# The end of a two-stage transformer kernel, ordered by hand: a change to the last two of 96 units

## The chip, the cores and the metric

One core of one Trainium2 chip. The metric is the device time of one execution in microseconds (us). The engines are TensorE (PE), VectorE (DVE), ScalarE (ACT), GpSimd (POOL) and SyncE (SP, which here issues DMAs only).

## The reference, cut to what matters

```python
def reference(...):          # x is (4, 512, 128) float32
    x = x + attention(layernorm(x), Wq, Wk, Wv, Wr)     # 16 heads of 64, penalty -50 above the diagonal
    x = x + layers(layernorm(x), ...)                   # six layers, as follows
    return x

for i in range(6):
    x = attn_layer(shift_tokens(x), Wqkv[i], q_scale[i], k_scale[i], Wo[i]) + x
    x = ffn_layer(shift_tokens(x), ln_g[i], ln_b[i], W1[i], b1[i], W2[i], b2[i]) + x

def attn_layer(...):         # q and k: norm per head, scale, rotary; windows of 32 queries
    ...                      # see their own and the previous 32 keys; softmax; product with V; Wo

def ffn_layer(x, ...):
    xn = (x - mu) / sqrt(var + 1e-05) * g + bln
    a, gate = split(xn @ W1 + b1)                       # 341 and 341 columns
    return a * gelu(gate) @ W2 + b2
```

`shift_tokens` takes the upper 64 of the 128 features from the token before. A batch is 512 tokens, that is 4 tiles of 128.

## The kernel before, in words

The order of instructions is the order in which the Python code issues them: the body runs under `tc.manual_schedule()`, each engine works off its own queue in that order, and semaphores, placed by the framework, hold an instruction until its data are there and its buffer is free.

The first stage (global attention) runs until about 560 us (its last transposes of probabilities, L315, start at 557 us). The second stage is cut into 96 units: 6 layers x 4 batches x 4 tiles of 128 tokens. `slot(n, ...)` issues one step of a software pipeline: for unit n the scores, exponents, their transposes, the product with V (`times_v`, in two halves) and the transposes of its result (`transpose_o`); for unit n-1 the product with Wo (`project_out_2`) and the residual; for unit n+1 the transposes of q and k; for unit n+2 the projections and norms. The feed-forward part of a batch (`Ffn`) is spread over seven slots behind the batch's last residual: `shift`, `mean`, `var`, `scale` (the layer norm), three GEGLU chunks of 128, 128 and 85 of the 341 columns, and `out` (the product with W2 and the residual). In the last layer `out` ends with `finish`: the sum with the first stage's output (`x1T`), four transposes, a copy and the output DMA. The loop runs on to slot 102, so the last slots hold ever less work: slot 94 and 95 belong to the last two units, 96 to 102 to the last batch's feed-forward alone.

Lines of before that are spoken of below: L80 to L86, the reciprocal square root by three Newton steps (4 instructions each, `rsqrt`), on VectorE for the feed-forward norms; L94 to L98 mean, subtraction and square; L103 the variance (products with one column); L111 the broadcast of the inverse root by transposes; L115, L117 the scaled result hT; L147 to L149 the shift by one token on GpSimd; L513 and L521 GpSimd's rotary sum and scaling; L585, L588 transposes and their copies by ScalarE; L604 the carry of 32 keys on GpSimd; L612, L623 scores (mask, then products); L633, L635 maximum and subtraction; L641 exponents; L655 the product with V; L664, L665 its division; L680, L688 product with Wo and residual; L713, L714 the two products of a GEGLU chunk (gate, value); L716 Gelu; L718 the gate's multiplication; L727 and L729 product with W2 and residual; L738, L741, L743, L744 the sum, transposes, copy and DMA of `finish`. ScalarE loads a function table (ACT_TABLE_LOAD) when it goes from exponents to Gelu or back.

PSUM: `one_t` hands out two banks in turn (transposes, means, variances, Wo products); `two_t(k)` hands out three pairs of banks, counted from `part[0]`. A taker waits until the former content of its bank has been read.

Of the kernel before, what the change touches and what calls it, by code (L numbers as in the profile page):

```python
# [15 lines left out]
P = 128  # L16
# [16 lines left out]
def body(ctx: ExitStack, tc: tile.TileContext, a, out: bass.AP):  # L33
# [41 lines left out]
    def rsqrt(v, n, eng):  # L75

        y = small.tile([P, n], F32, tag=f"y{n}", name="y")
        t = small.tile([P, n], F32, tag=f"yt{n}", name="yt")
        ti = t.bitcast(I32)
        nc.vector.tensor_scalar(ti, v.bitcast(I32), 1, None, ALU.logical_shift_right)  # L80
        nc.vector.tensor_scalar(y.bitcast(I32), ti, -1.0, 1597463007.0, ALU.mult, ALU.add)  # L81
        for k in range(3):
            eng.tensor_tensor(t, y, y, ALU.mult)  # L83
            eng.tensor_tensor(t, t, v, ALU.mult)
            eng.tensor_scalar(t, t, -0.5, 1.5, ALU.mult, ALU.add)
            eng.tensor_tensor(y if k < 2 else v, y, t, ALU.mult)  # L86

    def layernorm_steps(state, bank, inT, outT, g=None, b=None, eng=nc.vector):

        def mean():
            m = bank()
            mm(m, lhsT=avg, rhs=inT(), start=True, stop=True)  # L94
            xc = state["xc"] = tmpt()
            nc.vector.tensor_tensor(xc, inT(), m, ALU.subtract)
            sq = state["sq"] = tmpt()
            nc.scalar.activation(sq, xc, AF.Square)  # L98

        def var():  # L100
            v = bank()
            for t in range(NT):
                mm(v[:, t : t + 1], lhsT=state["sq"][:, t * P : (t + 1) * P], rhs=avg[:, 0:1], start=True, stop=True)  # L103
            rs = state["rs"] = small.tile([P, NT], F32, tag="rs", name="rs")
            nc.vector.tensor_scalar(rs, v[:, 0:NT], EPS, None, ALU.add)
            rsqrt(rs, NT, eng)

        def scale():
            bc = bank()
            for t in range(NT):  # L110
                nc.tensor.transpose(  # L111
                    bc[:, t * P : (t + 1) * P], state["rs"][:, t : t + 1].to_broadcast([P, P]), ident
                )
# [31 lines left out]
    def shift_into(dst, src):  # L145
# [3 lines left out]
        nc.gpsimd.tensor_copy(dst[HD:P, 1:S], src[HD:P, 0 : S - 1])  # L149
# [543 lines left out]
    class Ffn:  # L693
        def __init__(self, i, b):
            self.i, self.b, self.us, self.st = i, b, [], {}
# [4 lines left out]
                lambda: s2.tile([P, S], F32, tag="hT", name="hT", bufs=2),  # L700
                vecs[:, i, 0:1],
                vecs[:, i, 1:2],
            )

        def shift(self):
            self.xs = tmpt()
            shift_into(self.xs, xT[self.b])

        def chunk(self, f):
            i, (f0, fn), h = self.i, FCH[f], self.st["h"]  # L710
            w1 = ffn_w[0][0]
            gp = two_t(0, "ps_proj")
            mm(gp[0:fn, 0, :], lhsT=w1[:, DH + f0 : DH + f0 + fn], rhs=h, start=True, stop=True)  # L713
            mm(gp[0:fn, 1, :], lhsT=w1[:, f0 : f0 + fn], rhs=h, start=True, stop=True)  # L714
            g = tmpt()
            nc.scalar.activation(g[0:fn, :], gp[0:fn, 0, :], AF.Gelu, bias=vecs[0:fn, i, 6 + f : 7 + f])  # L716
            u = tmpt()
            nc.vector.scalar_tensor_tensor(  # L718
                u[0:fn, :], gp[0:fn, 1, :], vecs[0:fn, i, 3 + f : 4 + f], g[0:fn, :], ALU.add, ALU.mult
            )  # L720
            self.us.append(u)

        def out(self):
            w2 = ffn_w[0][1]
            y = two_t(0, "ps_proj")[:, 0, :]
            for f, (f0, fn) in enumerate(FCH):
                mm(y, lhsT=w2[0:fn, f, :], rhs=self.us[f][0:fn, :], start=(f == 0), stop=(f == len(FCH) - 1))  # L727
            xn = new_xT()
            nc.vector.scalar_tensor_tensor(xn, y, vecs[:, self.i, 2:3], xT[self.b], ALU.add, ALU.add)  # L729
            xT[self.b] = xn  # L730
            if self.i + 1 == L:
                self.finish(xn)
            elif self.b + 1 == B:
                ffn_w[0] = load_ffn(self.i + 1)

        def finish(self, xn):
            fin = tmpt()
            nc.vector.tensor_tensor(fin, x1T[self.b], xn, ALU.add)  # L738
            op = one_t()
            for t in range(NT):  # L740
                nc.tensor.transpose(op[:, t * P : (t + 1) * P], fin[:, t * P : (t + 1) * P], ident)  # L741
            ot = tmpt()
            nc.scalar.copy(ot, op)  # L743
            nc.sync.dma_start(  # L744
                out=out[self.b].rearrange("(t p) e -> p t e", p=P),
# [57 lines left out]
    def slot(n, now, last):  # L803
# [4 lines left out]
        T = n % NT  # L808
# [20 lines left out]
        if now and T > 0:  # L829
            (now.mean, now.var, now.scale)[T - 1]()  # L830
        if now and T == 0:
            now.shift()
# [34 lines left out]
        if now and T == 3:  # L867
            now.chunk(0)
        if last:
            (lambda: last.chunk(1), lambda: last.chunk(2), last.out)[T]()  # L870
# [3 lines left out]
    with tc.manual_schedule():  # L874
        begin(units[0])
        ffns = {}
        late = norm_x1(one_t, B - 1)
        first_slot()
        for n in range(-1, len(units) + NT + 3):
            if 1 <= n < 4:  # L880
                late[n - 1]()
            q = n // NT - 1
            if n % NT == 0 and 0 <= q < L * B:
                ffns[q] = Ffn(units[n - 1].i, units[n - 1].b)
            slot(n, ffns.get(q), ffns.pop(q - 1, None) if n % NT == 2 else ffns.get(q - 1))
# [93 lines left out]
```

## Time and profile before

| what | value |
|---|---|
| median of 3 runs (lowest, highest) | 2278.62 us (2278.29, 2281.74) |
| profiled execution | 2281.5 us, span of its instructions 2279.7 us |
| mean granted TensorE clock | 0.993 |
| busy PE, PEld, DVE, ACT, POOL | 2178.0, 1435.6, 1729.1, 1347.6, 1451.3 us |
| chain that ended last | PE 63%, DVE 9%, issue 2%, ACT 1% |
| last copy of a result ends | 2276.5 us; its DMA is issued at 2276.5 us |

The page cuts the span into 40 slices of 57 us. PE's digit is 9 in all but the first and the last, where it is 7. A PE that is "busy" all the time isn't at its peak, since matmuls are pipelined; but in the second stage little other than PE's own order ends waits. The span starts with the first instruction; 1.8 us of the execution lie around it.

### The profile page before, as it was taken

Reading aid. Unit: us, or ns where it says so; the run is one execution under the profiler, and the core shown is the slowest. Engines: PE = TensorE matmul, PEld = TensorE weight load, DVE = VectorE, ACT = ScalarE, POOL = GpSimd, SP = SyncE. Lnnn points to the kernel's source line nnn. Section 1 sums busy time; section 2 is a strip of 40 time slices with the busy share of each in tenths; the row PEclk is TensorE's granted clock in tenths of the full one; section 3 lists DMA queues with packets and bytes.
Section 4 is the critical chain, followed back from the end, with each engine's and each line's share of the span. In section 5 each row is a group of like instructions: output and inputs, shape, how many; then the busy total and the mean of one; then the engine's idle time right before and its main releaser. Section 6 shows DMA issues by size and latency. Waiting matters only on the chain.

```text
span 2279.7 us, 82205 instructions
## 1 busy us (share of the span) xinstructions
PE 2178.0 (96%) x35088; PEld 1435.6 (63%) x35088; DVE 1729.1 (76%) x2800; ACT 1347.6 (59%) x2550; POOL 1451.3 (64%) x1981
## 2 busy tenths in 40 slices
PE   6999999999999999999999999999999999999997
PEld 3555555555566666666666666666666666666664
DVE  3776667767778787878887788878888878888774
ACT  3665655655455656666566666666656666666562
POOL 1544545455877677767677777677776667766760
PEclk8999999999999999999999999999999999999998
DMA  3000000000322233232322323222332223222220
GB/s 115 1 1 1 1 1 1 1 1 1 75 70 64 63 88 75 58 75 68 87 67 64 77 70 91 64 62 69 85 85 56 72 63 88 73 67 70 65 56 15
DMA packets 91029, 125.74 MB, mean 55 GB/s; under 512 B 25390, under 2 KB 39468, under 8 KB 90668
## 3 DMA queue, kind: packets, MB, share of 16 engines
q1 hardware_dynamic: 90236, 118.92, 21.1%
q8 instruction: 279, 4.57, 0.9%
q10 hardware_dynamic: 432, 1.57, 0.2%
q14 instruction: 82, 0.67, 0.1%
HBM read 20.31 MB, written 1.05 MB: 9 GB/s over the span
## 4 chain that ended last, share of the span: by engine, by line
PE 63%; DVE 9%; issue 2%; ACT 1%; POOL 0%; POOLq 0%; ACTq 0%
PE ps_proj L477 19%; PE ps_one L585 14%; PE ps_one L680 7%; PE ps_att L655 6%; PE ps_att L623 6%; PE ps_proj L713 3%; PE ps_proj L714 3%; PE ps_proj L727 2%; DVE yt L80 2%; DVE t L502 1%; DVE rot L498 1%; PE ps_att L612 1%; PE ps_one L94 1%; PE ps_one L103 1%; DVE yt L83 1%
## 5 line engine op out<-in xcount | busy, mean ns | idle before, releaser
L513 POOL TENSOR_TENSOR rot<-rot,t 128x1024 f32<-128x1024 f32 x192 | 453.8, 2364 | 197.5 <-DVE t L502 185.9
L477 PE MATMUL ps_proj<-wqkv,xs 128*128 128x512 f32 x1152 | 553.3, 603 | 4.3 <-DVE t L502 2.8
L304 POOL TENSOR_TENSOR pr<-pr,den 128x1024 f32<-128x1024 f32 x128 | 240.9, 1893 | 266.9 <-DVE den L301 258.6
L488 ACT ACTIVATE sq<-ps_proj 128x1024 f32<-128x1024 f32 x192 | 196.8, 1025 | 356.7 <-PE ps_proj L477 324.5
L521 POOL TENSOR_TENSOR rot<-rot,ss 128x1024 f32<-128x1024 f32 x192 | 365.2, 1902 | 14.9
L477 PEld LDWEIGHTS ps_proj<-wqkv,xs 128*128 128x128 f32 x1152 | 198.1, 190 | 166.1 <-issue 146.5
L493 DVE TENSOR_REDUCE ss<-sq 128x16 f32<-128x1024 f32 x192 | 233.1, 1214 | 46.9 <-ACT sq L488 46.3
L498 DVE TENSOR_TENSOR rot<-ps_proj,lt 128x1024 f32<-128x1024 f32 x192 | 233.6, 1217 | 0.0
L502 DVE TENSOR_TENSOR t<-ps_proj,lt 128x1024 f32<-128x1024 f32 x192 | 233.2, 1215 | 0.4 <-POOL rot L513 0.4
L290 ACT ACTIVATE pr<-ps_sc,nm 128x128 f32<-128x128 f32 (+3 forms) x448 | 220.1, 507 | 20.0 <-DVE nm L279 16.7
L279 DVE TENSOR_REDUCE nm<-ps_sc 128x2 f32<-128x1024 f32 x128 | 156.0, 1219 | 91.0 <-PE ps_sc L267 91.0
L585 PE MATMUL ps_one<-ident,rot 128*128 128x128 f32 x1536 | 211.3, 280 | 5.9 <-issue 4.4
L680 PEld LDWEIGHTS ps_one<-aT,wo 128*128 128x128 f32 x1536 | 186.3, 192 | 45.3 <-issue 44.5
L83 POOL TENSOR_TENSOR yt<-y 128x32 f32<-128x32 f32 (+1 forms) x309 | 72.9, 236 | 210.5 <-DVE y L81 194.3
L633 DVE TENSOR_REDUCE mx<-ps_att 128x16 f32<-128x1024 f32 x96 | 117.5, 1224 | 102.3 <-PE ps_att L623 102.2
L680 PE MATMUL ps_one<-aT,wo 128*128 128x128 f32 x1536 | 187.3, 275 | 0.4 <-ACT aT L588 0.4
L585 PEld LDWEIGHTS ps_one<-ident,rot 128*128 128x128 f32 x1536 | 165.3, 141 | 25.3 <-issue 7.1
L319 ACT COPY pT<-ps_pt 128x512 f32<-128x512 f32 x128 | 75.5, 590 | 176.2 <-PE ps_pt L315 176.2
L655 PEld LDWEIGHTS ps_att<-vw,pT 64*32 64x32 f32 x9216 | 103.5, 105 | 93.4 <-ACT pT L588 54.0
L567 ACT COPY vt<-ps_proj 128x512 f32<-128x512 f32 x192 | 103.2, 590 | 93.6 <-PE ps_proj L477 91.6
L315 PEld LDWEIGHTS ps_pt<-ident,pr 128*128 128x128 f32 x1024 | 117.6, 142 | 56.7 <-issue 47.6
L655 PE MATMUL ps_att<-vw,pT 64*32 64x65 f32 x9216 | 129.0, 225 | 24.2 <-DVE t L502 13.4
(134 smaller groups left out, 4062.3 us busy)
## 6 DMA issues: line engine op xcount, KB each, us to landing
vw<-vt SPq DMA_DIRECT2D x1152, 65.0 KB
vw_first<-vt SPq DMA_DIRECT2D x336, 65.0 KB
wqkv<-in_wqkv_dram SPq DMA_DIRECT2D x18, 512.0 KB
wo<-in_wo_dram SPq DMA_DIRECT2D x6, 512.0 KB
w<-in_w_dram SPq DMA_DIRECT2D x6, 341.0 KB
xr<-in_x_dram SPq DMA_DIRECT2D x4, 256.0 KB
out_dram<-tmp_t SPq DMA_DIRECT2D x4, 256.0 KB
w<-in_w_dram SPq DMA_DIRECT2D x12, 64.0 KB
```

The costliest lines, as they stand in the source:

```text
L290: nc.scalar.activation(self.pr[:, h, cols], self.sc[:, h, cols], AF.Exp, bias=self.nm[:, part_, h : h + 1], accum_out=self.den[:, part_, h ...
L304: nc.gpsimd.tensor_tensor(self.pr, self.pr, self.den[:, 0].unsqueeze(2).to_broadcast([P, 2, S]), ALU.mult)
L477: mm(p[:, c, :], lhsT=u.xs[:, u.T * P : (u.T + 1) * P], rhs=wpart[j][:, c * 512 : (c + 1) * 512], start=True, stop=True,)
L488: nc.scalar.activation(u.sq, u.p[j], AF.Square)
L493: nc.vector.tensor_reduce(u.ss[:, j * HEADS : (j + 1) * HEADS], heads(u.sq), AX.X, ALU.add)
L498: nc.vector.tensor_tensor(heads(t0), heads(pf), lt[:, u.T, 2 * j].unsqueeze(1).to_broadcast([P, HEADS, HD]), ALU.mult)
L502: nc.vector.tensor_tensor(t1.rearrange("p (h t d) -> p h t d", t=2, d=half), pf.rearrange("p (h t d) -> p h t d", t=2, d=half)[:, :, ::-1, :],
L513: nc.gpsimd.tensor_tensor(u.r[j], u.r[j], u.t1, ALU.add)
L521: nc.gpsimd.tensor_tensor(heads(u.r[j]), heads(u.r[j]), u.ss[:, j * HEADS : (j + 1) * HEADS].unsqueeze(2).to_broadcast([P, HEADS, HD]), AL ...
L585: nc.tensor.transpose(tp[:, c * P : (c + 1) * P], src[:, (4 * g + c) * P : (4 * g + c + 1) * P], ident)
L655: mm(o[j * W : (j + 1) * W, h, c * (HD + 1) : (c + 1) * (HD + 1)], lhsT=u.pT[h * HD : (h + 1) * HD, 4 * g + c, j * W : (j + 1) * W], rhs=u ...
L680: mm(y[:, 0:P], lhsT=wo_w[0][:, c, :], rhs=u.aT[:, c, :], start=(c == 0), stop=(c == NC - 1))
```

## The change

Slots -1 to 93 issue what they issued before (but for the sum in `out`, which is now written in place). Slot 94 changes, and what follows is written out in `tail()`:

- In slot 94 the `out` of batch index 1 moves from the end of the slot to just behind the variance of batch index 2 (`plan(norm, end - 2, seq.var, ...)`). The scores of unit 95 come at that slot's end (`early_scores`), ahead of the result transposes (`finish`) of batch index 1 and of `transpose_o` of unit 94.
- The inverse root of batch index 2's norm, and those of the last batch, run on GpSimd (two integer instructions of each stay on VectorE).
- Batch index 2 (`seq`): its first GEGLU chunk comes right behind unit 95's product with V, its first gate behind that unit's divisions and result transposes; chunks 1 and 2 come later, `out` and `finish` later still.
- The last batch is cut in two: `most`, its first three tiles (384 columns), normed while unit 95 is at work, and `last`, the fourth tile (128 columns), normed between the chunks. The fourth tile's shift is two copies on ScalarE.
- Output: `finish` is split from `out`; the last three result transposes come last. The last batch's output is two DMAs, of 3 tiles and of 1.

The diff at its core:

```diff
-    def layernorm_steps(state, bank, inT, outT, g=None, b=None, eng=nc.vector):
+    def layernorm_steps(state, bank, inT, outT, g=None, b=None, eng=nc.vector, nt=NT, temp=tmpt):
...
-        def __init__(self, i, b):
+        def __init__(self, u, t0=0, nt=NT, temp=tmpt, pair=None, eng=None):
...
         def shift(self):
-            self.xs = tmpt()
-            shift_into(self.xs, xT[self.b])
+            n, c0 = self.nt * P, self.t0 * P
+            xs, src = self.temp()[:, 0:n], self.u.xn
+            if c0 == 0:
+                shift_into(xs, src[:, 0:n], n)
+            else:
+                nc.scalar.copy(xs[0:HD, :], src[0:HD, c0 : c0 + n])
+                nc.scalar.copy(xs[HD:P, :], src[HD:P, c0 - 1 : c0 + n - 1])
+            self.xs = xs
...
+            def gate():
+                nc.vector.scalar_tensor_tensor(
+                    u[0:fn, :], gp[0:fn, 1, 0:n], vecs[0:fn, i, 3 + f : 4 + f], g[0:fn, :], ALU.add, ALU.mult
+                )
+
+            if apart:
+                return gate
+            gate()
...
-        def finish(self, xn):
-            fin = tmpt()
-            nc.vector.tensor_tensor(fin, x1T[self.b], xn, ALU.add)
-            op = one_t()
+        def finish(self):
+            n, nt, t0, xn = self.nt * P, self.nt, self.t0, self.xn
+            op = one_t()[:, 0:n]
...
+        third, seq = f, Ffn(units[end - NT - 1], eng=nc.gpsimd)
+        plan(norm, end - 4, seq.shift)
+        plan(norm, end - 3, seq.mean)
...
+        most = Ffn(units[end - 2], 0, NT - 1, big, halves, nc.gpsimd)
+        last = Ffn(units[end - 1], NT - 1, 1, big, sixths, nc.gpsimd)
+        u, prev = units[end - 1], units[end - 2]
+
+        def early_scores():
+            part[0] = 0
+            scores(u)
+
+        plan(norm, end - 2, seq.var, *geglu.pop(end - 2))
+        plan(geglu, end - 2, early_scores, third.finish)
+
+        def tail():
+
+            exponents(u)
+            seq.scale()
+            project_out_2(prev)
+            residual(prev)
+            most.shift()
+            transpose_p(u)
+            most.mean()
+            part[0] = 1
+            times_v(u, 0)
+            times_v(u, 1)
+            part[0] = 0
+            gate = seq.chunk(0, 0, True)
+            transpose_o(u)
+            gate()
+            most.var()
+            project_out_2(u)
+            residual(u)
+            last.shift()
+            seq.chunk(1, 1)
+            last.mean()
+            most.scale()
+            last.var()
+            seq.chunk(2, 2)
+            for k in range(2):
+                most.chunk(k, k)
+            last.scale()
+            most.chunk(2, 2)
+            seq.out(0, True)
+            for k in range(3):
+                last.chunk(k, (k + 1) % 3)
+            seq.finish()
+            most.out(1, True)
+            last.out(2, True)
+            most.finish()
+            last.finish()
+
         first_slot()
-        for n in range(-1, len(units) + NT + 3):
+        for n in range(-1, end - 1):
             if 1 <= n < 4:
                 late[n - 1]()
...
+            slot(n, norm.get(n, ()), geglu.get(n, ()))
+        tail()
```

`third` is batch index 1 (its feed-forward is the third from the end), `seq` batch index 2. The chunks' and norms' tiles of the last batch live in buffers of the projections that are idle by then (`big`, `halves`, `sixths`).

## The prediction

> **What bounds the kernel now.** I read the busy shares and slices first, then the built order of both kernels, then stage windows, clock, chain and timeline of the end. Every instruction and wait before TensorE's L103 of the second-to-last unit (it ends at 2219.80 us) is the same in both, but for one addition written in place. So only 2219.80 to 2279.7 can change: the 17.0, 14.2, 25.5 and 3.2 us of these windows (columns after the two times' sum: PE, PEld, DVE, ACT, POOL busy; last but two the granted clock):
>
> ```profile
> 2219.80:2236.80 17.00, 14.04 (x308) 10.38 (x308) 8.59 (x22) 6.02 (x10) 3.93 (x4) 0.80 0.06 17
> 2236.80:2251.00 14.20, 10.71 (x185) 8.59 (x186) 6.34 (x10) 5.06 (x7) 0.00 (x0) 1.00 0.01 2
> 2251.00:2276.50 25.50, 19.72 (x56) 8.41 (x54) 11.03 (x28) 5.22 (x8) 1.21 (x2) 0.93 0.03 10
> 2276.50:2279.70 3.20, 0.00 (x0) 0.00 (x0) 0.00 (x0) 0.00 (x0) 0.00 (x0) 0.60 0.27 82
> ```
>
> PE is busy 44.5 of 59.9 us; elsewhere it is near 99%. The chain shows where it is late (start, length, what):
>
> ```profile
> 2230.45 0.76 DVE xT L729
> 2231.23 0.70 DVE tmp_t L738
> ...
> 2243.89 1.60 issue
> 2245.49 0.45 PE ps_att L655 x25
> ...
> 2264.01 2.08 PE ps_proj L713 x2
> 2266.09 1.33 PE ps_proj L714 x2
> ```
>
> Result transposes stand in PE's queue ahead of the next work and wait for VectorE (1.66 us before 2232.07, 2.13 before 2261.56); the last batch's hT lets PE idle 1.36 us before 2264.01. A second loss is the clock:
>
> ```profile
> 2223.00:2223.50 0.50, 0.50 (x38) 0.50 (x37) 0.47 (x2) 0.00 (x0) 0.50 (x2) 0.50 0.00 0
> 2235.00:2235.50 0.50, 0.50 (x54) 0.50 (x41) 0.00 (x0) 0.16 (x1) 0.00 (x0) 0.50 0.47 142
> 2264.00:2265.00 1.00, 0.99 (x1) 0.50 (x2) 0.00 (x0) 0.00 (x0) 0.00 (x0) 0.50 0.70 222
> ```
>
> It is 0.50 in three spells: 2222.5 to 2225.6, 2232.8 to 2236.3, 2263.5 to 2266.5. So L655 took 1.98 us instead of 0.86, and L713 with L714 3.2 instead of 1.72.
>
> **What the Trainium skill says.** "TensorE: Matmul & The Clock Gate", Part 1: a free-running window of 3413 ns with too little activity is followed by half clock. The trace agrees: the spells' starts are 10.2 and 30.7 us apart, 3.0 and 9.0 such windows, and each follows a stretch with idle time and transposes. "ScalarE: Activation LUTs", What ACT_TABLE_LOAD costs: about 1283 ns; here 1283 (L716, x67), hidden in the end (2242.21, its Gelu at 2247.89). "GPSIMD Engine Reference", Specifications: VectorE instructions with two SBUF inputs contend with GpSimd. Here too:
>
> ```profile
> 2220.05 1.36 DVE L80 TENSOR_SCALAR yt<-rs 128x4 int32<-128x4 int32 x1
> 2221.65 1.74 DVE L83 TENSOR_TENSOR yt<-y 128x4 f32<-128x4 f32 x1
> ```
>
> They last until GpSimd's L513 and L521 end.
>
> **The change, part by part.** Durations: 128x512 product 0.86, so 384 columns 0.65; 128 columns 0.233 (L680: 8 in 1.86); transpose 0.11; N=1 product 0.24; PE's last issue to the reader's start 0.28; VectorE 0.69 (two tensors), 0.75 (gate), 0.55, 384 columns less 0.13; ACT copy 0.59, Gelu 0.69.
>
> *Slot of the second-to-last unit.* L727's product goes behind L103, where PE was idle 0.99 us. From 2219.80: 2.58 (product), 0.44 + 0.28 (first transposes), 0.59 + 0.04 (copy), L655 0.86, q 0.88, L655 0.86, k 0.88: 2227.3. kT's copies add 0.4, the moved-up scores 1.95 (0.34 + 1.61): 2229.6, against 2236.76. The 7.2 us are the late transposes' wait and order (2.2), VectorE's 12-step square root that held L664 to 2225.64, and two cold spells. On GpSimd the 12 steps (200 ns each and 80 gap, 3.3) stand behind L513, L521, L604, from about 2223.7 to 2227.3; the reader, L111's broadcast, comes near 2231. L80 and L81 on VectorE still meet GpSimd (up to 3.1 us); cover: the next L664 is due at 2224.9, they end by 2223.5. The first result's DMA of 256 KB has nothing behind it on SP.
>
> *To the last product with V.* Max, subtract, exp, transpose and copy: 5.0 us from the scores in before (2236.76 to 2241.75). Now 6.8: project-out and residual of unit 94 lie inside, GpSimd's memset and two shift copies (0.47 each) end near 2235.4, and the mean's 0.65 product stands ahead of L655: 2236.4. Two L655 1.72, chunk 0 1.72: 2239.8, against 2247.6 (where 2.25 us were slow or stalled issue).
>
> *The added wait.* Chunk 0's Gelu here has its table load behind the wait for PE (before: none ahead of the load). Queued behind on ACT: Gelu and both aT copies; PE's variance product needs the first copy's bank, the last project-out both. 2239.8 + 0.28 + 1.28 + 0.69 + 0.55: 2242.6; variance 0.72, the rest of the copies 0.45, project-out 1.86: 2245.6, against 2250.97. Bounds of the load: 0 (if it ran early) and 1.28; I take 1.28.
>
> *Rest.* PE in order: chunk 1 1.72; last mean 0.23; broadcast 0.35; wait 1.9 for the last square (ACT, behind chunk 1's Gelu, its gate and L96's subtraction on VectorE); variance 0.24; chunk 2 1.72; three chunks of 384 columns 3.87 with a 0.4 wait for GpSimd's last 12 steps and one transpose 0.11; W2 of batch 2 2.58; three chunks of 128 columns 1.40 + 0.14; transposes 0.44 + 0.27; W2 1.93 and 0.70; wait 0.84 for VectorE's residuals; transposes 0.33 + 0.37 + 0.11; 0.28 and a last 128-column copy 0.27. The first three tiles' 12 steps on GpSimd (3.3) lie under project-out and chunk 1 (1.86 + 1.72); without that cover they would be on the path. Sum 20.2: 2265.8, against 2276.49; before needed 25.5. The split into 384 and 128 columns adds only 0.25 of PE, two ACT shift copies (0.3 each, on the last residual's path but beside chunk 1), one DMA: 192 and 64 KB for 256, both behind an idle SP; from the copy's end to the span's end 3.2 us were, I take 3.0 (bounds 2.5 and 3.4).
>
> *Cold windows.* Those 2265.8 are at full clock. I laid 3.41 us windows over this time line at many phases[...]. Between 0 and 3 are cold (mostly after PE's gap at 2240.7 to 2242.6), worth 0 to 4.6 us, 2.3 on average. Stalled issue: 3.6 us in the last 180, so 0.3 to 1.6; I take 0.7. End of copies 2268.8, of the span 2271.8, against 2279.7: 7.9 us off the profiled execution of 2281.5 gives 2273.6. That execution is 2.9 above the median of 2278.62 and within the runs (2278.29 to 2281.74), which spread 3.4, as cold phases would make them. Two of the three runs may have a kind phase already, so I take 7.3: **2271.3**.
>
> **Rivals.** *Second form of the gain: kind phase.* No window cold, no stall: 2265.8 + 0.3 + 3.0 makes 10.6 off the profiled span, about 10 off the median: 2268.5. For it: PE has few gaps; against: two of 1.9 us. *New gaps eat it.* Three cold windows (4.6) and a stall of 2.2 in the dense run L655, transposes, L655, scores: 2265.8 + 6.8 + 3.2, so 3.9 off: 2274.7. For it: the 1.6 us stall and three spells in before. *Not what it says:* if the end were bound by ACT or VectorE in order, moving PE's work would gain only the first wait, 1.7: 2276.9. Against: their busy shares after 2219.8 are 16.3 and 26.0 of 56.7 us. *Slower:* the gap at the table load puts PE at half clock and the narrow chunks and transposes never wake it: after 2242.6 that adds 16 us (PE's 18.3 us of work after it doubled, the rest of them beside waits), so 2278.6 - 9.6 + 16 = 2285. It decides from some 10 us of half-clock PE work, three windows on end; against it: each spell in before ended after one window.
>
> **How the numbers follow.** About 0.2% (4.6 us) is what a measurement can tell from no change. Forecast 0.55 (2269.5 to 2273.5), kind phase 0.15, new gaps 0.20 (half of it beyond 2274.1), not what it says 0.07, slower 0.03. Faster: 0.55 + 0.15 + 0.10 = 0.80; same 0.10 + 0.07 = 0.17; slower 0.03. Range 2268.0 to 2275.2: it leaves out the last two cases and the ends of the second and third.
>
> **What would show it.** Right: the last unit's scores end near 2229.6; no 1.7 us wait of PE for L738's tile; chunk 0's table load directly ahead of its Gelu with PE idle about 1.9 us near 2241; last project-out's end near 2245.6; last copy 20 to 23 us after it. Wrong: scores not before 2233; clock 0.50 over more than three windows; last 12-step root on GpSimd over 4 us; a wait for PSUM banks or output DMAs among the last chunks.

## The result, and the profile after

The changed kernel takes 2272.39 us (median of five runs), the kernel before 2280.53 us beside it (six runs, the three of the table above among them). A sixth run of the changed kernel, 3648.61 us at a mean granted clock of 0.674, lies far off in a throttled state of the chip and is left out (with it the median is 2272.95). The ratio is 0.9965, with a 95% interval of 0.9951 to 0.9978: 8.1 us between the medians, between 5.0 and 11.2 by the interval. The forecast was 2271.3 and a gain of 7.3.

The profiled execution of the changed kernel is its fastest: 2270.65 us, span 2268.9, 10.8 us under the profiled span of before. In the changed kernel's code the lines of the root stand 1 further down than before (L81 to L87) and those from L97 to L691 stand 3 further down; the chunks' products are now L726 and L727, their Gelu L730, the gate L734, W2 L746, residual and sum L749 and L751, result transposes and their copy L764 and L766. Windows of the kernel after, in the columns of the windows of before: to the end of the last unit's scores, to the end of the last project-out, to the last copy, to the end of the span.

```profile
2219.80:2230.40 10.60, 10.32 (x298) 7.56 (x298) 4.05 (x11) 4.28 (x7) 5.84 (x16) 1.00 0.01 3
2230.40:2246.50 16.10, 13.45 (x205) 10.34 (x205) 7.45 (x14) 7.34 (x11) 2.13 (x8) 1.00 0.06 19
2246.50:2265.90 19.40, 16.64 (x67) 9.44 (x65) 9.65 (x23) 6.35 (x14) 3.48 (x19) 1.00 0.05 14
2265.90:2268.90 3.00, 0.00 (x0) 0.00 (x0) 0.00 (x0) 0.00 (x0) 0.00 (x0) 0.63 0.28 87
```

The same checkpoints took 17.0, 14.2, 25.5 and 3.2 us before: the scores' stage is 6.4 us shorter, the middle 1.9 longer (it now holds more work), the last stretch 6.1 shorter. The clock is 1.00 until the last copy. TensorE's timeline after (start, length, what; in brackets the idle time ahead of a group and what ended it) has only these waits over 0.3 us:

```profile
2236.46 0.91 PE L97 MATMUL ps_one<-rot,avg 128*128 128x384 f32 x2 [0.45 <-POOL rot L152]
...
2243.38 0.83 PE L106 MATMUL ps_one<-avg,rot 128*128 128x1 f32 x6 [1.72 <-ACT aT L591]
...
2250.40 0.38 PE L106 MATMUL ps_one<-avg,rot 128*128 128x1 f32 x2 [1.61 <-ACT rot L101]
...
2264.60 0.98 PE L764 MATMUL ps_one<-ident,rot 128*128 128x128 f32 x4 [0.64 <-DVE rot L751]
```

In the kernel before there were these (two more, 0.99 for L641's exponents at 2220.80 and 0.38 at 2249.11, are not printed):

```profile
2232.07 0.63 PE L741 MATMUL ps_one<-ident,tmp_t 128*128 128x128 f32 x4 [1.66 <-DVE tmp_t L738]
...
2240.43 1.09 PE L585 MATMUL ps_one<-ident,pr 128*128 128x128 f32 x8 [1.25 <-ACT pr L641]
...
2245.49 0.45 PE L655 MATMUL ps_att<-vw,pT 64*32 64x65 f32 x28 [1.60 <-issue]
...
2261.56 0.66 PE L741 MATMUL ps_one<-ident,tmp_t 128*128 128x128 f32 x4 [2.13 <-DVE tmp_t L738]
...
2264.01 2.08 PE L713 MATMUL ps_proj<-hT,w 128*128 128x512 f32 x2 [1.36 <-DVE hT L117]
...
2275.24 0.63 PE L741 MATMUL ps_one<-ident,tmp_t 128*128 128x128 f32 x4 [1.66 <-DVE tmp_t L738]
```

The 5.45 us that result transposes waited for VectorE's sum are down to 0.64; 1.25 before the transposes of probabilities and 1.36 before the last batch's chunk 0 are gone. In their place stand two new holes, 1.72 and 1.61. The first is the one that the table load makes; ScalarE's timeline after:

```profile
2240.87 1.28 ACT L730 ACT_TABLE_LOAD   x1 [2.35 <-PE ps_proj L727]
2242.17 0.69 ACT L730 ACTIVATE tmp_t<-ps_proj,vecs 128x512 f32<-128x512 f32 x1
```

ScalarE has been idle for 2.35 us when the load starts, and chunk 0's product has just ended, at 2240.79: the load didn't use the idle time, it came only after the wait.

**A balance of the end.** From here on each profile is read by one stretch: from the start of the eight one-column products of batch index 2's variance (L103, after L106) to the end of ScalarE's last copy. It is split into four terms: time lost to half clock (over windows of half a microsecond, TensorE's busy time by one minus the granted clock), TensorE's idle time put down to stalled issue (the profile shows nothing that it waited for), its idle time put down to a releaser, that is, to the instruction whose end let it go on (waits), and what is left, its work at full clock and the last copy.

| profile | stretch | half clock | stalled issue | waits | rest |
|---|---|---|---|---|---|
| before | 57.63 | 4.82 | 1.60 | 9.91 | 41.30 |
| after | 46.80 | 0.00 | 0.00 | 5.15 | 41.65 |
| difference | -10.83 | -4.82 | -1.60 | -4.76 | +0.35 |

The rest came out at 41.3 to 42.0 us in every profile of this study (but for one kernel with work added), so little but the first three terms varies. The 0.25 forecast for the narrower chunks can't be seen in it: the two profiles of before alone differ by 0.41 in the rest (the second is below). The terms can hide each other, as one experiment below shows: what another engine finishes during a stall or during slow work at half clock is no wait afterwards. More than half of what these two profiles differ by, 6.42 us, is clock and stall, not waits.

### The profile page after: what moved, and what is told of

It is laid out like the page before. It is cut to its first block, busy times and chain, and to the rows that moved or that the text cites. A ratio compares the mean times of both kernels' runs of the same rounds, so it can differ in the third digit from the quotient of the medians.

```text
span 2268.9 us, 82280 instructions
## 1 busy us (share of the span) xinstructions
PE 2174.1 (96%) x35108; PEld 1436.5 (63%) x35108; DVE 1724.6 (76%) x2787; ACT 1348.9 (59%) x2557; POOL 1458.3 (64%) x2017
## 3 DMA queue, kind: packets, MB, share of 16 engines
q1 hardware_dynamic: 90252, 118.92, 21.1%
q10 hardware_dynamic: 432, 1.57, 0.2%
## 4 chain that ended last, share of the span: by engine, by line
PE 63%; DVE 9%; issue 2%; ACT 1%; POOL 0%; ACTq 0%; POOLq 0%
PE ps_proj L480 19%; PE ps_one L588 13%; PE ps_one L683 7%; PE ps_att L658 6%; PE ps_att L626 6%; PE ps_proj L746 3%; PE ps_proj L726 3%; PE ps_proj L727 3%; DVE t L505 2%; DVE yt L81 2%; DVE rot L501 2%; PE ps_att L615 1%; PE ps_one L97 1%; PE ps_one L106 1%; DVE yt L84 1%
## 5 line engine op out<-in xcount | busy, mean ns | idle before, releaser
L293 ACT ACTIVATE pr<-ps_sc,nm 128x128 f32<-128x128 f32 (+3 forms) x448 | 220.1, 507 | 19.7 <-DVE nm L282 16.7
L84 POOL TENSOR_TENSOR yt<-y 128x32 f32<-128x32 f32 (+2 forms) x318 | 74.7, 235 | 222.4 <-DVE y L82 205.5
L683 PEld LDWEIGHTS ps_one<-aT,wo 128*128 128x128 f32 x1536 | 186.4, 192 | 45.0 <-issue 44.4
L683 PE MATMUL ps_one<-aT,wo 128*128 128x128 f32 x1536 | 187.3, 275 | 0.3 <-DVE rs L108 0.3
L658 PEld LDWEIGHTS ps_att<-vw,pT 64*32 64x32 f32 x9216 | 102.4, 105 | 92.8 <-ACT pT L591 53.5
L658 PE MATMUL ps_att<-vw,pT 64*32 64x65 f32 x9216 | 127.9, 225 | 23.5 <-DVE t L505 14.5
```

The source lines that it names most:

```text
L293: nc.scalar.activation(self.pr[:, h, cols], self.sc[:, h, cols], AF.Exp, bias=self.nm[:, part_, h : h + 1], accum_out=self.den[:, part_, h ...
L658: mm(o[j * W : (j + 1) * W, h, c * (HD + 1) : (c + 1) * (HD + 1)], lhsT=u.pT[h * HD : (h + 1) * HD, 4 * g + c, j * W : (j + 1) * W], rhs=u ...
L683: mm(y[:, 0:P], lhsT=wo_w[0][:, c, :], rhs=u.aT[:, c, :], start=(c == 0), stop=(c == NC - 1))
```

## The experiments

Theory: TensorE's waits for VectorE and for the order of the work, and the half-clock windows that follow them, were the loss; the change removes most of them. Rivals: it is mostly the clock (and so the phase of an execution); it is VectorE relieved of the roots; it is the earlier scores.

Twelve kernels ran in three groups of four, each group on a chip of its own. The kernel before took 2285.15, 2285.69 and 2284.83 us (medians of 30, 20 and 24 runs) beside the first, second and third group. Intervals of the ratios reach 0.0006 to 0.0014 each way (1.4 to 3.2 us), so differences of medians under 3 us show little by themselves, and the balance carries the argument:

| profile | stretch | half clock | stalled issue | waits | rest | median us | ratio to before (95% interval) |
|---|---|---|---|---|---|---|---|
| before, again | 56.56 | 3.11 | 1.60 | 10.14 | 41.71 | 2285.00 | 1.0004 (0.9993, 1.0015) |
| after, again | 46.79 | 0.00 | 0.00 | 5.15 | 41.64 | 2275.61 | 0.9969 (0.9957, 0.9981) |
| before, waits filled | 58.97 | 3.25 | 3.70 | 4.41 | 47.61 | 2282.18 | 0.9987 (0.9981, 0.9994) |
| load early | 47.19 | 0.00 | 1.61 | 3.86 | 41.72 | 2272.67 | 0.9944 (0.9932, 0.9956) |
| chunk 2 ahead | 51.29 | 1.70 | 1.89 | 5.69 | 42.01 | 2277.55 | 0.9969 (0.9959, 0.9979) |
| both | 46.36 | 0.00 | 0.00 | 4.41 | 41.95 | 2272.18 | 0.9946 (0.9932, 0.9959) |
| scores late | 50.94 | 1.71 | 2.45 | 5.27 | 41.51 | 2278.93 | 0.9969 (0.9956, 0.9981) |
| roots on VectorE | 48.35 | 1.65 | 0.19 | 5.14 | 41.37 | 2273.74 | 0.9950 (0.9936, 0.9963) |
| chunk 0 behind transposes | 46.92 | 0.00 | 1.61 | 3.48 | 41.83 | 2271.66 | 0.9942 (0.9929, 0.9954) |
| one last batch | 55.08 | 3.98 | 0.00 | 9.24 | 41.86 | 2281.27 | 0.9984 (0.9977, 0.9991) |
| results not last | 51.41 | 1.63 | 0.00 | 8.24 | 41.54 | 2277.64 | 0.9971 (0.9962, 0.9979) |
| four edits | 45.84 | 0.00 | 0.00 | 4.01 | 41.83 | 2273.14 | 0.9954 (0.9941, 0.9966) |

**Both kernels again.** No edit; the third group's chip.

> The changed kernel unaltered, on the chip of the runs beside it, since the kernel before took 2285.2 and 2285.7 us beside the earlier experiments (2280.5 beside the changed kernel). If those 5 us are a common shift of both kernels (their shared part): 2277.5 to 2278. If they are of the kernel before alone (more half-clock windows at its end): 2272.5 to 2274.

> The kernel before unaltered, for a second profile of it on the same chip. If its 5 us lie at its end, the stretch from the variance of batch index 2 to the last copy takes 62 to 63 us here instead of 57.6; if they lie in the shared part, that variance starts near 2224 instead of 2218.9, and the stretch is 57 to 58 us.

After took 2275.61 beside 2284.83: neither 2278 nor 2273, but between. The ratio by runs is 0.9969; the two medians make 0.9960, inside its interval. Of the two readings for the kernel before, neither held cleanly: the variance starts at 2221.36 (2.5 us later than in the first profile, where 5 were needed) and the stretch is 56.56, no longer than before. Its profiled run of 2282.92 is below the median, so the slower ones aren't seen. In the shared part from 560 to 2215 us the stalled issue is 21.0 us here and was 19.3 in the first profile (after: 21.1 and 16.7), so part of the 5 us is there; the rest is open.

What the repeat does show: the waits of after come again to the hundredth (5.15), and so does the stretch without half clock and stall. Those of before come within 0.3 us. What differs most between the two executions of before is half clock (4.82 and 3.11); the rest differs by 0.41. The pair of this chip makes -9.77 = -3.11 (half clock) - 1.60 (stall) - 4.99 (waits) - 0.07. Both profiled runs of after are the fastest of theirs (2270.65 of 2270.65 to 2273.53; 2272.02 of 2272.02 to 2278.05), so the zero half clock may be the kind case; a median gain of 8 to 9 beside 10 to 11 between profiles fits that, but no slower run of after has a profile.

**The waits of before, filled.** Products that nobody reads, in front of each group of result transposes and of the last batch's chunk 0; its result transposes are L745.

```diff
             op = one_t()
+            for k in range(2):
+                mm(op, lhsT=ident, rhs=ffn_w[0][0][:, 0:S], start=True, stop=True)
...
             gp = two_t(0, "ps_proj")
+            if f == 0 and i + 1 == L and self.b + 1 == B:
+                mm(gp[:, 0, :], lhsT=ident, rhs=w1[:, 0:S], start=True, stop=True)
```

> The kernel before, with products nobody reads put into TensorE's waits at the end: two of 512 columns ahead of each of the three groups of result transposes of the last layer and one ahead of the last batch's chunk 0 (6.0 us of work in holes of 1.7, 2.1, about 1.5 and 1.4 us). They leave every wait's length as it is and only keep TensorE active. If half-clock windows are a large part of what the change removed: the three spells of the kernel before go, 2 to 4 us off, 2277. My prediction's share for the clock is about 2 us of 7.3 (waits and order the rest): 2278.5. If the change gained by waits and order alone: 2280.5, or up to 1 us more where a filler overruns its hole.

2282.18 against 2285.15; 0.9987, so 1.4 to 4.3 us faster, with 6 us of useless work added. Nothing that TensorE waits for comes earlier by this, so the clock is the candidate for these 3 us. TensorE's timeline shows the fill in the hole:

```profile
2227.62 1.88 PE L743 MATMUL ps_one<-w,ident 128*128 128x512 f32 x4
2229.36 0.66 PE L745 MATMUL ps_one<-ident,tmp_t 128*128 128x128 f32 x4
...
2261.66 0.66 PE L745 MATMUL ps_one<-ident,tmp_t 128*128 128x128 f32 x4 [0.41 <-DVE tmp_t L740]
```

The waits fell from 9.91 and 10.14 to 4.41 and the rest rose by 5.9 to 6.3: without half clock and stall the stretch is 52.02 us for 51.21 and 51.85, so the fills kept it nearly as it was. The half clock of this one profile (3.25) is no smaller than in before's second; its first spell, from about 2219.9, begins before any filler, its second, from 2243.9, follows stalls of 2.04 and 1.66 us, and none follows directly on a fill. The profile doesn't place the gain at the end: its stretch of 58.97 is longer than both of before, and what is shorter is the shared part (the variance starts at 2216.13, in before at 2218.86 and 2221.36). The mean granted clock of all runs is higher with the fills, 0.998 over 22 runs for 0.995 over the 30 runs of before beside them, but it counts idle time, and the first 35 us, where an execution can be at half clock too (0.50 from 20 to 30 us in the first profile of before, 1.00 in its second). So that clock is a part of the gain, 3 of 8 to 9 us, is what the median suggests and no profile here shows; that it is all of it falls, since the waits alone make 4.8 to 5.0 us between the profiles.

**The table load early.** After, with a Gelu of one column behind the copies of probabilities.

```diff
             transpose_p(u)
+            nc.scalar.activation(small.tile([P, 1], F32, tag="warm", name="warm"), ident[:, 0:1], AF.Gelu)
             most.mean()
```

> The changed kernel with a one-column Gelu on ScalarE behind the copies of the last unit's probabilities, so that the function table is loaded while ScalarE has nothing to do; chunk 0's Gelu then follows its product at once. Theory (the load is on the path): TensorE's wait before the variance of the last batch's first three tiles falls from 1.72 us to about 0.45, the last project-out ends 1.3 us earlier (2245.2 against 2246.5 in the changed kernel's profile), the median 1.0 to 1.3 us under the changed kernel's 2273.0: 2271.8. Rival (the load is hidden by the divisions and transposes behind it, the wait is another's): wait unchanged within 0.3 us, 2273.0.

ScalarE's timeline of this kernel:

```profile
2238.62 1.28 ACT L948 ACT_TABLE_LOAD   x1
2239.92 0.20 ACT L948 ACTIVATE warm<-ident 128x1 f32<-128x1 f32 x1
...
2244.47 0.69 ACT L730 ACTIVATE tmp_t<-ps_proj,vecs 128x512 f32<-128x512 f32 x1 [3.94 <-PE ps_proj L727]
```

and the wait of TensorE behind it:

```profile
2245.69 0.83 PE L106 MATMUL ps_one<-avg,rot 128*128 128x1 f32 x6 [0.44 <-ACT aT L591]
```

1.72 became 0.44, as the theory says: 1.28 us of the load were on the path. The stretch without stall is 45.58, 1.2 under that of after. The median of 2272.67 lies 2.9 under the 2275.61 of after on another chip, more than the 1.3. The ratio's interval, 0.9932 to 0.9956, just misses that of after's repeat and overlaps that of its first measurement (0.9951 to 0.9978), so the size of the gain in time is open. Half clock could add to it: behind the 1.72 us hole the next products (L683, 2.05 us at full clock) took 3.62 and 3.57 us at half clock in two of seven profiles that have the hole, and 2.79 in a third; in the four profiles without it they never did. That is the window that the prediction placed "mostly after PE's gap".

**Chunk 2 ahead of the last tile's variance**, alone and with the load early.

```diff
-            last.var()
             seq.chunk(2, 2)
+            last.var()
```

> The changed kernel with chunk 2 of batch index 2 ahead of the last tile's variance in TensorE's order. Theory (TensorE's order sets the end; the 1.6 us wait for the last tile's square is a plain hole): the hole goes, 1.4 to 1.6 us off, 2271.5. Rival (the last tile's norm is itself the path, so that putting it back by 1.7 us opens a hole later, ahead of its chunks or the copy of hT): no gain, 2273.0, with a new wait of 1 us or more before 2262.

> Both edits together: early table load and chunk 2 ahead of the last tile's variance. Theory: the two holes add, 2.7 to 2.9 us off the changed kernel, 2270.2, and fewer half-clock windows. Rival (one of them only moves the wait on): at most 1.5 us off, 2271.5 or more.

Alone:

```profile
2265.98 0.32 PE L114 MATMUL ps_one<-ident,rs 128*128 128x128 f32 x1 [1.95 <-POOL rs L87]
```

The 1.61 us hole is gone, and 1.95 us appear before the last tile's broadcast: its root on GpSimd takes its 3.2 us and starts 1.1 us later than in after (1.89 us of stall ahead of it taken out), because VectorE's step before it (L108, at 2262.13) now stands behind chunk 2's gate (L734, at 2261.47). The waits are 5.69 for 5.15 alone, and 4.41 for 3.86 together with the early load. The rival is right: the fourth tile's norm is itself a path, and filling a hole in front of it only moves it. The theory that the two holes add falls. The two kernels here differ by the early load alone, and their medians by 5.4 us on one chip (2277.55 and 2272.18); the waits account for 1.3 of that, and what the rest is stays open. The profile of chunk 2 ahead is of its slowest run.

**Scores late.** After, with the last unit's scores put behind batch index 1's result and the transposes of the products with V.

```diff
-        plan(geglu, end - 2, early_scores, third.finish)
+        plan(geglu, end - 2, third.finish)
...
         def tail():
 
+            early_scores()
             exponents(u)
```

> The changed kernel with the last unit's scores put back behind the transposes of batch index 1's result and of the unit before's products with V; all else as changed. Theory (2.2 us of the lead at the scores' end come from the late transposes' wait and order): TensorE then waits about 1.0 to 1.7 us for VectorE's sum ahead of the result transposes, and scores end about 2 us later than 2230.3; the median rises by 1.5 to 2.5 us over the changed kernel's 2273.0, to 2275.0. Rival (the early scores only move a wait, since the exponents that follow are covered by project-out): within 0.5 us, 2273.3. Other rival (the exponents lose all their cover): 3.5 us more, 2276.5.

The waits are 5.27 for 5.15, and the stretch without half clock and stall is 46.78 for 46.80. The wait for VectorE's sum did not come back: with `out` moved ahead, the sum is done when the result transposes come (0.29 us of wait there, put down to a copy of kT). That the exponents fit under project-out is owed to a stall, though:

```profile
2237.92 0.27 PE L114 MATMUL ps_one<-ident,rs 128*128 128x128 f32 x1 [1.08 <-issue]
2238.03 1.95 PE L683 MATMUL ps_one<-aT,wo 128*128 128x128 f32 x16
...
2238.92 1.06 ACT L644 ACTIVATE pr<-pr 128x1024 f32<-128x1024 f32 x1 [3.55 <-DVE pr L638]
...
2240.03 1.09 PE L588 MATMUL ps_one<-ident,pr 128*128 128x128 f32 x8
```

The exponents end at 2239.98, and the transposes of the probabilities start at 2240.03, as soon as project-out is through. Without the 1.08 us of stall ahead of it project-out would have ended about 1 us earlier, and TensorE would have waited that long for the exponents; before, where the scores stand as late, it waited 1.25 us for them. So the early scores are worth about 1 us of wait, by this estimate: neither the theory's wait nor nothing, as the rival has it. The median is 5 and 7 us above the next two kernels of its group all the same; in its profile 4.2 us are stall and half clock and the shared part ends 2.7 us late. Whether later scores cause these or chance did, one profile can't tell; the time stays open.

**Roots on VectorE.** After, with the default engine for `seq`, `most` and `last`.

```diff
-        third, seq = f, Ffn(units[end - NT - 1], eng=nc.gpsimd)
+        third, seq = f, Ffn(units[end - NT - 1])
...
-        most = Ffn(units[end - 2], 0, NT - 1, big, halves, nc.gpsimd)
-        last = Ffn(units[end - 1], NT - 1, 1, big, sixths, nc.gpsimd)
+        most = Ffn(units[end - 2], 0, NT - 1, big, halves)
+        last = Ffn(units[end - 1], NT - 1, 1, big, sixths)
```

> The changed kernel with the inverse roots of the last two batches back on VectorE. My prediction said that VectorE's 12 steps held the division behind the product with V of the second-to-last unit (to 2225.6 before), so in the first root about 1 us of wait of TensorE returns at 2224 to 2226; the two later roots (12 steps of about 0.1 to 0.17 us, 1.5 us in all, against 3.3 on GpSimd) are shorter on VectorE. Theory: net 0 to 1.0 us slower, 2273.5. Rival (the move to GpSimd is what made the gain): 3 us or more slower, 2276. Rival (GpSimd's roots cost, being slower): 1 us faster, 2272.

The waits are 5.14 for 5.15: nothing. VectorE's timeline has the old long steps again:

```profile
2221.66 1.33 DVE L81 TENSOR_SCALAR yt<-rs 128x4 int32<-128x4 int32 x1
...
2223.23 1.75 DVE L84 TENSOR_TENSOR yt<-y 128x4 f32<-128x4 f32 x1
...
2228.61 0.20 DVE L667 RECIPROCAL rden<-ps_att 128x8 f32<-128x8 f32 x1
```

The division (L667) comes at 2228.61, 8.1 us after the start of the variance, where after has it 6.5 after (2225.53 from 2219.08), and TensorE has no wait for it: the next reader, the transposes of the result, stands behind the scores. So the move of the roots brought nothing to TensorE's waits.

**Chunk 0 behind the transposes.** After, without its first two steps.

```diff
-            gate = seq.chunk(0, 0, True)
             transpose_o(u)
-            gate()
+            seq.chunk(0)
```

> The changed kernel with chunk 0 behind the transposes of the last unit's products with V, and its gate right behind it (so neither 'chunk behind the last product with V' nor 'gate behind the divisions'). Theory: TensorE waits for the last division ahead of the transposes (0.28 + about 0.8 us, less what it did in chunk 0's 1.72), but the transposes' copies now run ahead of the table load: the load hides behind them and project-out comes sooner; net 0 to 1 us slower, 2273.5. Rival (this step is the main gain): 2 us or more slower, 2275. Rival (the load's place makes the step a loss): 0.5 us or more faster, 2272.4.

TensorE's timeline, and ScalarE's:

```profile
2242.55 0.66 PE L588 MATMUL ps_one<-ident,on 128*128 128x128 f32 x4 [0.52 <-DVE on L668]
2243.04 1.02 PE L726 MATMUL ps_proj<-hT,w 128*128 128x512 f32 x2
...
2250.51 0.54 PE L114 MATMUL ps_one<-ident,rs 128*128 128x128 f32 x3 [1.20 <-POOL rs L87]
```

```profile
2243.24 0.59 ACT L591 COPY aT<-ps_one 128x512 f32<-128x512 f32 x1 [0.54 <-PE ps_one L588]
2243.85 1.28 ACT L730 ACT_TABLE_LOAD   x1
2245.14 0.69 ACT L730 ACTIVATE tmp_t<-ps_proj,vecs 128x512 f32<-128x512 f32 x1
```

Without chunk 0 as cover TensorE waits 0.52 us for the division, and then no more before the variance: the copies run ahead of the load, and variance and project-out follow without a hole (1.72 and 0.25 before). Later it waits 1.20 for the root of the first three tiles, which is held by chunk 0's gate on VectorE (the gate ahead of L108 waits for load and Gelu until 2245.86). The waits are 3.48 for 5.15; the stretch without stall is 45.31, 1.5 under after and the shortest of all. (The stall of 1.37 us here stands ahead of the divisions and hides no wait: in the last kernel below, with the same order and no stall, the wait for the division is 0.49.) The third reading (the load's place makes the step a loss) holds in the waits. The ratio's interval, 0.9929 to 0.9954, lies under that of after's repeat (0.9957 to 0.9981) and overlaps that of its first measurement (0.9951 to 0.9978).

**One last batch.** After, without the cut in 384 and 128 columns: the norm of all four tiles begins behind the last residual.

```diff
-        most = Ffn(units[end - 2], 0, NT - 1, big, halves, nc.gpsimd)
-        last = Ffn(units[end - 1], NT - 1, 1, big, sixths, nc.gpsimd)
+        whole = Ffn(units[end - 1], 0, NT, big, halves, nc.gpsimd)
...
             residual(u)
-            last.shift()
+            whole.shift()
             seq.chunk(1, 1)
-            last.mean()
-            most.scale()
-            last.var()
             seq.chunk(2, 2)
-            for k in range(2):
-                most.chunk(k, k)
-            last.scale()
-            most.chunk(2, 2)
+            whole.mean()
             seq.out(0, True)
-            for k in range(3):
-                last.chunk(k, (k + 1) % 3)
+            whole.var()
             seq.finish()
-            most.out(1, True)
-            last.out(2, True)
-            most.finish()
-            last.finish()
+            whole.scale()
+            for k in range(3):
+                whole.chunk(k, (k + 1) % 3)
+            whole.out(1)
```

> The changed kernel without the cut of the last batch: its norm of four tiles starts behind the last residual, among chunks 1 and 2 and the product with W2 of batch index 2, and its three chunks of 512 columns, W2, transposes and one DMA of 256 KB come last. Theory: shift, mean, subtraction, square, variance, root on GpSimd and scaling take about 11 us from the last residual, TensorE has 8.3 us of other work for them, so a hole of 2.5 us; 0.25 us less TensorE work; longer last residual, sum and copy (0.6 more): 2.5 to 3.5 us slower, 2276.0. Rival (the cut gains nothing since there is enough other work): within 0.7 us, 2273.3. Rival (the cut is the main gain): 5 us or more, 2278.

The waits are 9.24 for 5.15, half clock 3.98, the median 2281.27: about half of the gain is lost or more (0.9984 for 0.9969), and no other edit of after brings so many waits. TensorE's timeline and the windows around the hole (PE's busy time first, the granted clock third from the right):

```profile
2259.56 1.12 PE L114 MATMUL ps_one<-ident,rs 128*128 128x128 f32 x4 [3.24 <-POOL rs L87]
2262.03 2.07 PE L726 MATMUL ps_proj<-hT,w 128*128 128x512 f32 x2 [1.36 <-DVE hT L120]
...
2274.74 1.09 PE L764 MATMUL ps_one<-ident,xT 128*128 128x128 f32 x4 [1.66 <-DVE xT L751]
```

```profile
2253.50:2257.50 4.00, 2.03 (x14) 1.46 (x12) 1.85 (x5) 0.59 (x1) 0.95 (x5) 1.00 0.00 0
2257.50:2267.60 10.10, 6.68 (x11) 3.19 (x12) 1.98 (x3) 0.69 (x1) 1.42 (x8) 0.51 0.08 27
```

Holes of 0.78 (result transposes), 3.24 (root) and 1.36 us (hT) make 5.4 on the way to the first chunk, for the 2.5 expected; the 1.36 and the last sum's 1.66 are those of before, back again. And here 10.1 us of half clock lie on end, about three of the 3.4 us windows that the Trainium skill describes ("TensorE: Matmul & The Clock Gate", Part 1): the mechanism of my slower rival, in a kernel with holes of 3.24 and 1.36 us close together. In neither profile of after did it show.

**Results not last.** After, with each group of result transposes behind its own product with W2.

```diff
             seq.out(0, True)
+            seq.finish()
             for k in range(3):
                 last.chunk(k, (k + 1) % 3)
-            seq.finish()
             most.out(1, True)
-            last.out(2, True)
             most.finish()
+            last.out(2, True)
             last.finish()
```

> The changed kernel with each batch's result transposes right behind its product with W2 (not last): those of batch index 2 ahead of the fourth tile's chunks, those of the first three tiles ahead of the fourth's product with W2. Theory: TensorE waits for VectorE's residual and sum twice, 0.28 + 0.75 + 0.69 us = 1.7 and 0.28 + 0.62 + 0.56 = 1.4, less the 0.8 it waited at the end: 2 to 2.5 us slower than the changed kernel beside it, the stretch from variance to last copy 49.0 for 46.8. Rival (VectorE and ScalarE bound the last microseconds, so the order of TensorE doesn't matter): within 0.5 us.

```profile
2264.74 0.66 PE L764 MATMUL ps_one<-ident,xT 128*128 128x128 f32 x4 [1.57 <-DVE xT L751]
...
2270.28 0.55 PE L764 MATMUL ps_one<-ident,rot 128*128 128x128 f32 x3 [1.30 <-DVE rot L751]
2270.67 0.83 PE L746 MATMUL ps_proj<-pr,w 128*128 128x128 f32 x6
2272.36 0.30 PE L764 MATMUL ps_one<-ident,rot 128*128 128x128 f32 x1 [0.86 <-DVE rot L751]
```

These are TensorE's last groups: 1.57, 1.30 and 0.86 in place of one wait of 0.64. The first two are the sums of the expectation (1.7 and 1.4), the third was left out there. The stretch without half clock is 49.78 for 46.80, so 3.0 longer; the median is 2.0 over after on the same chip, but the ratios by runs, 0.9971 and 0.9969, don't tell the two apart.

**Four edits that the profiles point to.**

```diff
-        last = Ffn(units[end - 1], NT - 1, 1, big, sixths, nc.gpsimd)
+        last = Ffn(units[end - 1], NT - 1, 1, big, sixths)
...
-            gate = seq.chunk(0, 0, True)
             transpose_o(u)
-            gate()
+            gate = seq.chunk(0, 0, True)
             most.var()
+            gate()
...
             last.mean()
+            seq.chunk(2, 2)
             most.scale()
             last.var()
-            seq.chunk(2, 2)
```

> The changed kernel with four edits that the profiles point to: chunk 0 behind the last transposes of products with V (so that the table load comes behind their copies), the variance of the last batch's first three tiles ahead of chunk 0's gate on VectorE, chunk 2 ahead of the first three tiles' broadcast and the fourth tile's variance, and the fourth tile's root on VectorE (1.2 us instead of 3.3). Theory (TensorE's waits of 1.72 and 1.61 us are what is left, and no other engine is near): the stretch from variance to last copy 43.8 to 44.5 instead of 46.8 without half clock or stalled issue, 2.3 to 3 us off the changed kernel beside it. Rival (the waits move to VectorE's work on hT or to the gates): 1 us off or less.

```profile
2254.60 0.91 PE L726 MATMUL ps_proj<-hT,w 128*128 128x384 f32 x2 [1.95 <-DVE hT L120]
```

The stretch is 45.84: 0.95 under after, not 2.3 to 3. One hole of 1.95 us stays. VectorE's timeline shows why:

```profile
2252.83 0.75 DVE L734 SCALAR_TENSOR_TENSOR tmp_t<-ps_proj,vecs,tmp_t 85x512 f32<-85x512 f32 x1 [1.01 <-ACT tmp_t L730]
2253.49 0.54 DVE L118 TENSOR_TENSOR hT<-rot,ps_one 128x384 f32<-128x384 f32 x1
```

The root was ready at 2250.48, but with chunk 2 ahead of the broadcast its gate (L734) is ahead of the scaling of hT in VectorE's queue, and the gate waits for Gelu. The rival holds. The median is 2.5 us under after's on the same chip (2273.14, 2275.61), with intervals that overlap: this version is not shown to beat after. Among all, chunk 0 behind the transposes with its 45.31 has the best case, though it ran on another chip than after. Moving batch index 1's `out` back alone was not tried.

## Why the prediction was right

- *Only the end can change.* Held: the variance starts at 2218.86 before and 2219.08 after. Over all profiles it starts between 2216.13 and 2227.34, so the shared part varies by more than the gain.
- *Scores end at 2229.6.* 2230.33. The miss is one term: L658's first group at 0.86; it took 1.67 at a clock of 1.00 (and 1.67 in the second profile of before, at full clock too). The row I had read, 1.98 against 0.86, was put down to the clock alone.
- *The 7.2 us of lead: late transposes and order 2.2, VectorE's root, two cold spells.* The wait of the late transposes and the two cold spells are gone in this execution. The root was a wrong term: with it on VectorE again the waits are the same, and TensorE did not wait for the division (L664) before either. Its waits there up to the scores are 0.99 and 0.24 us for the exponents and the copy of their transposes and 1.66 for the sum; the transposes that read the division start at 2232.53, and the second division ended at 2227.77. The early scores take about 1 us away, but at the exponents and not at the scores' end.
- *GpSimd's 12 steps from 2223.7 to 2227.3.* 2222.79 to 2226.53, one step of 0.65 among those of 0.20, while VectorE ran L751. The 3.1 us allowed for L80 and L81 were 0.26 for the one that met GpSimd.
- *Chunk 0 ends at 2239.8.* 2240.8: 0.7 us from the scores and 0.3 more on the way.
- *The added wait: 1.28 of the load, TensorE idle about 1.9.* 1.72 idle; the early load took away 1.28. The step is right to the hundredth, and it is the price of the change's own step of putting chunk 0 right behind the product with V: chunk 0 behind the transposes had no such price.
- *Project-out ends at 2245.6, last stretch 20.2, last copy 2265.8 at full clock.* 2246.5, 19.4 and 2265.88. The sum hits by luck: the 0.9 late were made up by waits below the estimate (1.61 for 1.9 at the last square, 0.64 for 0.84 at the last sum; no wait for the last root).
- *Copy to span's end 3.0.* 3.02.
- *Cold windows 2.3, stalls 0.7 on average.* None in this execution, which is the prediction's kind phase. The other four undisturbed runs are 0.3 to 2.9 us longer, and all five average 1.6 above this one, about half of the 3.0 allowed; only this one of them has a profile, so what made the others longer isn't seen.
- *The gain of 7.3 as against 7.9.* I took 0.6 off since the profiled run of before lay 2.9 over its median. With three more runs before's median became 2280.53, so the profiled run lies only 1.0 over it, and that of after 1.7 under its own. The gain between medians is 8.1; the level of 2271.3 is 1.1 low, less than the 1.9 by which before's median rose. How close the number came is in part luck, then: a wrong term (the root), a product taken at 0.86 for 1.67, waits and cold windows estimated too long, which cancel.

Of the rivals, *kind phase* describes both profiled runs of after but not its medians; *new gaps* is real in the two holes of 1.72 and 1.61, which were in the sum already; *not what it says* falls with the waits (5.15 for 9.91).

What stays open: why the kernel before takes 4 to 5 us more beside the three later groups than beside the first result, how much of the gain in time is clock, and whether the stalled issue belongs to a program or to chance. Both profiles of before stall 1.60 us at the same product of the last unit (L655, behind its 100th), both of after nowhere there, five of the other kernels 1.37 to 1.66 in the same product. So 1.6 of the profiles' 10 us may have nothing to do with the change's idea.

## What to carry to other kernels

Where one engine is full and works in a fixed order, split a profile's end into half clock, stalled issue, waits and work: four terms that add up tell more than medians with 3 us of spread, as long as each stall is looked at for a wait that it hides (1.08 us of stall hid about 1 us here). When a step is moved to fill a hole, it must be followed on each engine that it uses: here a function table's load (1.28 us), a gate and a root each moved into the hole's place. What took away most waits was to give the last piece its latency early (the cut of the last batch), and to ask for results of another engine last.

## What the runs showed of the hardware

- A table load (1.28 us) can run in idle time or not: before it did, at 2242.21 for a Gelu at 2247.89; in after the same load came only behind 2.35 us of idle ScalarE, directly ahead of its Gelu; with a one-column Gelu ahead it ran in idle time again, at 2238.62. What decides this was not tested.
- Half clock does not follow every hole: after the same 1.72 us hole the next 16 products took 2.05 us in four profiles, 2.79 to 3.62 in three.
- VectorE's two small steps of a root ran 1.33 and 1.75 us for 0.17 while GpSimd worked on 128x1024 operands, again and again (1.36 and 1.74 before, 0.53 and 1.74 in its repeat), and ended with GpSimd's instruction. The Trainium skill ("GPSIMD Engine Reference", Specifications) names such a contention for VectorE instructions with two SBUF inputs or in a 2-port mode; the 1.75 us step (L84) has two inputs, the 1.33 us step (L81) has one, and no run here shows its mode. The other way, GpSimd's step took 0.65 for 0.20 beside VectorE's 128x512 sum.
